# Adding the last bias to the residual in the middle stage instead of the last, for 12 of 16 pairs

## Chip, cores and metric

One core of a Trainium2 chip runs the whole program. The metric is the device time of one execution in microseconds (us). The engines are named as in the profile: PE multiplies matrices, DVE, ACT and POOL (GpSimd) work on elements, SP issues most of the transfers. All data are fp32; several products run on fp32 split into a high and a low part.

## What is computed

The input x has 32 samples of 64 channels by 1024 positions. Two blocks follow each other, each adding a feed-forward network over a style-modulated convolution network to its input:

```python
x = x + ffn0(cond0(x, cond))          # ffn0: 64 experts of rank 16, top 16 by a router, softmax gates
x = x + ffn1(cond1(x, cond))          # ffn1: a linear layer with 4-bit weights

def cond(x, style, ...):              # four modulated convolutions of width 3:
    for i, typ in enumerate(('same', 'upsample', 'same', 'downsample')):
        x = layer(x, style, weights[i], biases[i], mod_w[i], mod_b[i], typ)
    return x

def ffn1(x, qweight, scales, zeros, bias):
    W = scales * nibbles(qweight) - zeros          # per output column
    return einsum('bsi,io->bso', x, W) + bias
```

The change is about the last line, `+ bias`, and the `x +` in front of it. The bias has 1024 values, one for each position, and is the same for all rows.

## The kernel before

Two samples make a pair: 128 rows (2 x 64 channels) by 1024 positions. There are 16 pairs and three stages.

The first stage (loop at L1347) computes `cond0` and the first half of `ffn0` of each pair and leaves the gated products in DRAM. The second, the middle stage (loop at L1412), turns the products of pair p+1 on PE (`turned_h`, L1070), multiplies those of pair p with the second expert matrix (`layer0b`, L1108; 48 matmuls of 512 columns for one pair, the last 16 of them with the difference tile `td`), and adds x. The result is `x1`, the input of the second block. It lies in an order split four ways by position, `(f j)`, position 4j+f standing at f*256+j, because the second convolution network needs it so. It goes to DRAM twice: whole to `x1d` (L1160) as the residual, and as four parts with differences to `x1e` (L1162, L1172) for the convolutions.

The last stage (loop at L1477) computes `cond1` for pair k+1 and k+2 beside the 4-bit product of pair k (`layer1`, L1194). For each pair `load_x1` (L1177) brings the residual back from `x1d` into a buffer `xb`. `with_bias` (L1183) then makes a second buffer `o` on POOL in one instruction of 128 x 1024 (L1187): residual plus bias, with the order turned back to plain. A one-element copy named `turn` (L1215) in front of it pins it behind a DVE instruction of the next pair's convolutions. At the end DVE adds the zeros' part to `o` (L1226) and scales each third of the product (L1228), POOL adds that to `o` (L1230), and `o` is stored.

What else the steps below touch:

- Buffers with the tag `w4` are [128, 1024] and there are three. In the middle stage they hold the loaded products `hg` and `x1`; in the last `xb` and `o`.
- Buffers with the tag `hi` are [128, 512], three too. `high` (L146) takes one whenever DVE cuts the high part of a tile: twice for each pair in the middle stage (`hh`, inside `split`, L915), twice in the last.
- `crossed` (L931) makes `td` on POOL (L935, 128 x 1024) from a pair's high and low parts. There is one such buffer, so that of pair p+1 can be written only when PE has ended pair p; it must be there when PE reaches the last third of pair p+1.
- `cv` is one large buffer that is cut by hand (L44 to L50). In the middle stage it first holds the second expert matrix (`braw`, 8 x 1024 columns), then the set-up of the second convolution network (`set1`, one step of it after each of the pairs 1 to 6), the residual x of the next pair (`load_residual`), and small tiles of `ends` (L449), which computes the outermost outputs of the second network after pairs 12 and 13. Its last 2 x 1152 columns, `fwv(0)` and `fwv(1)`, are the composed convolution weights, first used by the last stage's work at pair 14.
- The framework that builds the kernel orders each engine's instructions by its own estimate of when they are ready and by their place in the program; `tc.issue_after` pins one behind another. A buffer of a pool is given out when its first writer is placed, and the waits that this needs are added.

Of the kernel before, what the change touches and what calls it, by code (L numbers as in the profile page):

```python
# [8 lines left out]
F32 = mybir.dt.float32  # L9
# [3 lines left out]
ALU = mybir.AluOpType  # L13
AX = mybir.AxisListType

P = 128
# [4 lines left out]
NP = B // 2  # L21
L = 1024
# [3 lines left out]
H = 512  # L26
# [19 lines left out]
XD, XE, Y, FW = L + 4, 3 * HQ - 1, YE + 4 * P, 9 * P  # L46
O_XE = 2 * XD
O_Y = O_XE + 2 * XE
O_FW = O_Y + 2 * Y
CV = O_FW + 2 * FW  # L50
# [13 lines left out]
def adaln_ffn_kernel(ctx: ExitStack, tc: tile.TileContext, t, out: bass.AP):  # L64
    nc = tc.nc
# [25 lines left out]
    cv = const.tile([P, CV], F32, name="cv")  # L91
# [21 lines left out]
    eps = const.tile([P, 1], F32, name="eps")  # L113
    condT = const.tile([P, B], F32, name="condT")

    x1d = dram.tile([NP, P, 4, L // 4], F32, name="x1d")
    x1e = dram.tile([NP, P, 2, XE], F32, name="x1e")
    hgd = dram.tile([NP, P, L], F32, name="hgd")
    rowd = dram.tile([2, B, 2, C], F32, name="rowd")
# [2 lines left out]
    def xdv(n):  # L122
        return cv[:, (n % 2) * XD : (n % 2 + 1) * XD]
# [35 lines left out]
        return p > (4 if i == 0 else 1)  # L159

    DIRECT = 4


    def zeros_once():
# [489 lines left out]
                )  # L654
        return fw

    def clear(i):

        for n in range(2):
            if i == 0:  # L660
                nc.gpsimd.memset(xdv(n)[:, 0 : L + 3 : L + 2], 0.0)
            nc.gpsimd.memset(fwv(n)[C:, NT * C : 8 * C], 0.0)

    def clear_y(ys):
# [431 lines left out]
    def load_residual(p):  # L1096
        if p in WHOLE:
            v = tokens("tl", f"xres{p}", F32).rearrange("p a b -> p (a b)")
        elif p < NP - 1:
            v = cv[:, O_Y + Y : O_Y + Y + L]  # L1100
        elif p < NP:
            v = wk.tile([P, L], F32, tag="w4", name="xres", bufs=3)
        else:
            return
        nc.sync.dma_start(v, t["x"][p])
        residual[p] = v

    def layer0b(p, ws):  # L1108

        whole = p in WHOLE  # L1110
        key = f"h{p}"
        xres = residual.pop(p)
        x1 = wk.tile([P, L], F32, tag="w4", name=f"x1_{p}", bufs=3)
        x4 = x1.rearrange("p (f j) -> p j f", f=4)

        def banks(c):
            return [fpst(f"o{p}_{c}_{j}") for j in range(1 if whole else 2)]

        def joined(c, qd):
            cs = slice(c * H, (c + 1) * H)  # L1120
            v = xres[:, cs]
            if not whole:
                nc.vector.scalar_tensor_tensor(v, qd[1], -SCALING / RADIX, v, ALU.mult, ALU.add)  # L1123
            nc.vector.scalar_tensor_tensor(  # L1124
                x4[:, c * P : (c + 1) * P],
                qd[0].rearrange("p (j f) -> p j f", f=4),
                SCALING if whole else SCALING * (1.0 + 1.0 / RADIX),
                v.rearrange("p (j f) -> p j f", f=4),
                ALU.mult,
                ALU.add,  # L1130
            )

        cols = [slice(c * H, (c + 1) * H) for c in range(2)]
        if p == NP - 1:
            qds = [banks(c) for c in range(2)]

            for part in (Q, D):
                for k in range(4):
                    for ch in zip(qds, cols):
                        product(ch, key, ws, lambda k: k, part, (k,))  # L1140
            yield
            for ch in zip(qds, cols):
                product(ch, key, ws, lambda k: k, Q, range(4, NC))
                yield
            for c, ch in enumerate(zip(qds, cols)):
                product(ch, key, ws, lambda k: k, D, range(4, NC))
                joined(c, qds[c])
                if c == 0:
                    yield
        else:  # L1150
            qds = [banks(c) for c in range(2)]
            for ch in zip(qds, cols):
                product(ch, key, ws, lambda k: k, Q)
            for c, ch in enumerate(zip(qds, cols)):
                product(ch, key, ws, lambda k: k, D)
                joined(c, qds[c])
                yield
        if p not in WHOLE:
            load_residual(p + 1)
        nc.sync.dma_start(x1d[p].rearrange("p f j -> p (f j)"), x1)  # L1160
        v = x1.rearrange("p (f j) -> p f j", f=4)
        nc.sync.dma_start(x1e[p, :, :, : HQ - 1], v[:, :2])  # L1162
        dd = wk.tile([P, 4 * HQ], F32, tag="rt", name=f"dd{p}", bufs=1)
        dd = dd.rearrange("p (f j) -> p f j", f=2)
        nc.gpsimd.memset(dd[:, :, 0:1], 0.0)
        nc.vector.tensor_tensor(dd[:, :, 1:HQ], v[:, 2:], v[:, :2], ALU.subtract)
        nc.scalar.mul(dd[:, :, HQ : HQ + 1], v[:, :2, 0:1], -1.0)
        done["dd"] = nc.vector.tensor_tensor(
            dd[:, :, HQ + 1 : 2 * HQ - 1], v[:, 2:, : HQ - 2], v[:, :2, 1 : HQ - 1], ALU.subtract
        )  # L1170
        nc.scalar.copy(dd[:, :, 2 * HQ - 1 :], v[:, 2:, HQ - 2 : HQ - 1])
        nc.sync.dma_start(x1e[p, :, :, HQ - 1 :], dd)  # L1172
        v = x1.rearrange("p (f j) -> p j f", f=4)
        for s, js in enumerate((slice(0, 2), slice(L // 4 - 2, L // 4))):
            nc.gpsimd.tensor_copy(xg[:, p, s].rearrange("p (j f) -> p j f", f=4), v[:, js])

    def load_x1(p):  # L1177
        if p < NP:
            v = wk.tile([P, L], F32, tag="w4", name=f"xb_{p}", bufs=3)
            nc.sync.dma_start(v, x1d[p].rearrange("p f j -> p (f j)"))  # L1180
            residual[NP + p] = v

    def with_bias(p, aux):  # L1183

        if p < NP:
            o = residual[p] = wk.tile([P, L], F32, tag="w4", name=f"o1_{p}", bufs=3)
            nc.gpsimd.tensor_tensor(  # L1187
                o.rearrange("p (j f) -> p j f", f=4),
                residual.pop(NP + p).rearrange("p (f j) -> p j f", f=4),
                aux[:, 2].rearrange("p (j f) -> p j f", f=4),  # L1190
                ALU.add,
            )

    def layer1(p, wq, aux):  # L1194


        o = residual.pop(p)
        for c in range(3):
            if c == 0:
                load_x1(p + 1)  # L1200
            ps = fpst(f"q{p}_{c}")[:, :QC]
            for j, half in enumerate(toks[f"x1_{p}"]):
                for k in range(NC):
                    nc.tensor.matmul(  # L1204
                        ps,
                        half[:, k],
                        wq[at(k)][:, c * QC : (c + 1) * QC],
                        start=(k == 0 and j == 0),
                        stop=(k == NC - 1 and j == 1),
                    )  # L1210
                if j == 0:
                    if c == 1 and p + 1 < NP:

                        turn = tiny.tile([P, 1], F32, tag="turn", name=f"turn{p}")
                        v = nc.gpsimd.tensor_copy(turn, uppers[f"h1_{p + 1}_0"][:, :1])  # L1215
                        with tc.issue_after(v.ins):
                            with_bias(p + 1, aux)
                    yield
            a = 2 if c == 0 else 0
            cs = slice(c * QC + a - 2, (c + 1) * QC - 2)  # L1220
            if c == 0:
                nrs = tiny.tile([P, 1], F32, tag="nrs", name=f"nrs{p}")
                nc.vector.tensor_scalar_mul(nrs, ps[:, 0:1], -1.0)
            if c == (0 if p == NP - 1 else 2):
                with tc.issue_after(done["lo"].ins):
                    nc.vector.scalar_tensor_tensor(o, aux[:, 1], nrs, o, ALU.mult, ALU.add)  # L1226
            s = wk.tile([P, QC], F32, tag="yt", name=f"sc{p}_{c}", bufs=2)[:, : QC - a]
            nc.vector.tensor_tensor(s, ps[:, a:], aux[:, 0, cs], ALU.mult)  # L1228
            eng = nc.vector if p == NP - 1 and c == 2 else nc.gpsimd
            eng.tensor_tensor(o[:, cs], o[:, cs], s, ALU.add)  # L1230
            if p == NP - 1:
                nc.sync.dma_start(out[p][:, cs], o[:, cs])
            yield
        if p < NP - 1:
            nc.sync.dma_start(out[p], o)
# [66 lines left out]
            split_weights(araw, AW, (k,), wa, "wa")  # L1302

    nc.sync.dma_start(condT, t["condT"])
    clear(0)
    zeros_once()
    set0 = factors(0, *(block(k, [P, 3 * AW], F32, f"room{k}") for k in range(2)))
    next(set0)
# [103 lines left out]
    for p in range(NP):  # L1412
# [9 lines left out]
            begin(NP + 1)  # L1422
        if p <= len(WHOLE):
            load_residual(p)
        main = layer0b(p, braw if p in WHOLE else wb)
        next(main)
        if p in WHOLE:
            split_weights(braw, L, range(4 * p, 4 * p + 4), wb, "wb")
        if p == 7:
            clear(1)  # L1430
            clear_y([yv(0)])
        if p == LAST:
            load(NP)
            tables_of(NP)
            set_ends = ends(1, 0, LAST, cv[:, O_FW:])
        if p in (LAST, LAST + 1):
            next(set_ends)
        if p == NP - 2:
# [24 lines left out]
        run(main)  # L1463
        if p + 1 < NP:
            crossed(f"h{p + 1}")
        if 0 < p < 7:
            with tc.issue_after(done["td"].ins):
                next(set1, None)
# [75 lines left out]
```

## Time and profile before

| | us |
|---|---|
| median of 3 runs (lowest to highest) | 893.91 (893.53 to 894.51) |
| the profiled execution: span from its first to its last instruction | 893.1 |
| first stage, about | 0 to 407 |
| middle stage, about | 407 to 628 |
| last stage, about | 628 to 893 |

| busy us in | PE | DVE | ACT | POOL |
|---|---|---|---|---|
| 407 to 628 (221.0) | 217.2 | 162.3 | 72.4 | 84.0 |
| 628 to 893.1 (265.1) | 257.2 | 247.4 | 97.0 | 215.0 |

Times within the span are counted from its start. The page's first part gives each engine's busy time over the whole span. A table by windows gives it for stretches that one chooses, for instance one pair of a stage. The timeline lists instructions in order of time, with the idle time of the engine just before one, and what ended that, in square brackets. The 16 transfers of `x1d` out and the 16 back move 512 KB each.

### The profile page before, as it was taken

Reading aid. Unit: us, or ns where it says so; the run is one execution under the profiler, and the core shown is the slowest. Engines: PE = TensorE matmul, PEld = TensorE weight load, DVE = VectorE, ACT = ScalarE, POOL = GpSimd, SP = SyncE. Lnnn points to the kernel's source line nnn. Section 1 sums busy time; section 2 is a strip of 40 time slices with the busy share of each in tenths; the row PEclk is TensorE's granted clock in tenths of the full one; section 3 lists DMA queues with packets and bytes.
Section 4 is the critical chain, followed back from the end, with each engine's and each line's share of the span. In section 5 each row is a group of like instructions: output and inputs, shape, how many; then the busy total and the mean of one; then the engine's idle time right before and its main releaser. Section 6 shows DMA issues by size and latency. Waiting matters only on the chain.

```text
span 893.1 us, 14916 instructions
## 1 busy us (share of the span) xinstructions
PE 866.1 (97%) x5033; PEld 775.1 (87%) x5033; DVE 723.2 (81%) x1460; ACT 352.4 (39%) x817; POOL 531.1 (59%) x745
## 2 busy tenths in 40 slices
PE   6989999999999999999999999999999999999997
PEld 4876888999999999994688888888899999999997
DVE  4475898888888888778986765669999999999996
ACT  6444544444444444333332221247333433343340
POOL 7235654666666666556572222343787888888884
PEclk9999999999999999999999999999999999999999
DMA  8632222222232222345475666555543334334321
GB/s 240 155 73 54 54 69 62 88 89 80 79 91 83 81 79 71 106 178 149 139 232 193 201 193 197 189 192 167 164 117 111 98 100 143 114 90 139 122 66 71
DMA packets 49739, 109.81 MB, mean 123 GB/s; under 512 B 13700, under 2 KB 22400, under 8 KB 49664
## 3 DMA queue, kind: packets, MB, share of 16 engines
q1 hardware_dynamic: 48704, 107.88, 39.5%
q10 hardware_dynamic: 960, 0.99, 0.5%
q8 instruction: 40, 0.66, 0.3%
q14 instruction: 35, 0.29, 0.1%
HBM read 70.97 MB, written 37.88 MB: 122 GB/s over the span
## 4 chain that ended last, share of the span: by engine, by line
PE 42%; DVE 7%; POOL 2%; issue 2%; ACT 0%; DVEq 0%; POOLq 0%; ACTq 0%
PE o L955 16%; PE q L1204 11%; PE f L619 3%; PE r L875 3%; PE c L773 2%; PE r L834 1%; PE r L843 1%; PE c L768 1%; PE ht L1079 1%; PE g L596 1%; DVE cv L716 1%; DVE x L1124 1%; PE p L826 1%; DVE rt L866 1%; DVE r L884 0%
## 5 line engine op out<-in xcount | busy, mean ns | idle before, releaser
L716 DVE TENSOR_TENSOR cv<-cv 128x257 f32<-128x257 f32 x120 | 105.8, 913 | 1.3 <-ACT cv L758 0.9
L730 POOL TENSOR_TENSOR cv<-cv 128x256 f32<-128x256 f32 x120 | 77.7, 647 | 29.8 <-DVE cv L716 25.1
L722 POOL TENSOR_TENSOR cv<-cv 128x128 f32<-128x128 f32 x100 | 39.0, 411 | 67.5 <-PE r L843 48.3
L1204 PE MATMUL q<-wq,thx 128*128 128x342 f32 x384 | 73.0, 332 | 2.1 <-ACT thx L913 2.1
L955 PE MATMUL h<-wa,tdx 128*128 128x352 f32 (+1 forms) x336 | 72.2, 351 | 0.2 <-DVE wa L382 0.2
L1204 PE MATMUL q<-wq,tlx 128*128 128x342 f32 x384 | 72.3, 330 | 0.0
L619 PE MATMUL f<-gs,iw 128*128 128x128 f32 (+1 forms) x384 | 68.2, 327 | 0.1
L619 PEld LDWEIGHTS f<-gs,iw 128*128 128x128 f32 x384 | 61.8, 190 | 5.9 <-issue 0.5
L955 PE MATMUL h<-wa,thx 128*128 128x352 f32 (+1 forms) x336 | 64.7, 333 | 0.0
L1204 PEld LDWEIGHTS q<-wq,thx 128*128 128x128 f32 x384 | 60.3, 189 | 4.1 <-ACT thx L913 3.2
L770 ACT ACTIVATE yt<-c,be,al 128x257 f32<-128x257 f32 x56 | 31.7, 567 | 80.4 <-PE c L768 77.3
L875 PE MATMUL r<-cv 128*128 128x128 f32 x480 | 63.4, 274 | 0.0
L1204 PEld LDWEIGHTS q<-wq,tlx 128*128 128x128 f32 x384 | 61.9, 189 | 0.8
L955 PE MATMUL h<-wa,tlx 128*128 128x352 f32 (+1 forms) x336 | 62.4, 327 | 0.0
L955 PE MATMUL o<-wb,thh 128*128 128x512 f32 x224 | 60.4, 402 | 1.5 <-ACT wb L375 1.5
L935 POOL TENSOR_TENSOR tdx<-thx,tlx 128x1024 fp32r<-128x1024 f32 x14 | 34.7, 2479 | 44.5 <-ACT tlx L927 36.2
L955 PEld LDWEIGHTS h<-wa,tdx 128*128 128x128 f32 x336 | 56.9, 188 | 2.4 <-DVE wa L382 0.5
L1123 DVE SCALAR_TENSOR_TENSOR cv<-o,cv 128x512 f32<-128x512 f32 x26 | 18.0, 692 | 50.2 <-PE o L955 50.2
L955 PE MATMUL o<-wb,tlh 128*128 128x512 f32 x224 | 58.4, 397 | 0.0
L875 PEld LDWEIGHTS r<-cv 128*128 128x128 f32 x480 | 58.4, 191 | 0.0
L634 ACT COPY cv<-f 128x256 f32<-128x256 f32 x64 | 24.0, 375 | 83.9 <-PE f L619 46.3
L642 POOL TENSOR_TENSOR cv<-cv 128x256 f32<-128x256 f32 x60 | 50.0, 833 | 11.4 <-ACT cv L637 11.4
(313 smaller groups left out, 2274.6 us busy)
## 6 DMA issues: line engine op xcount, KB each, us to landing
cv<-in_x_dram SPq DMA_DIRECT2D x60, 256.0 KB
cv<-x1e SPq DMA_DIRECT2D x64, 192.5 KB
x1e<-dd SPq DMA_DIRECT2D x16, 514.0 KB
hgd<-hs SPq DMA_DIRECT2D x16, 512.0 KB
hg<-hgd SPq DMA_DIRECT2D x16, 512.0 KB
x1d<-x SPq DMA_DIRECT2D x16, 512.0 KB
xb<-x1d SPq DMA_DIRECT2D x16, 512.0 KB
out_dram<-o SPq DMA_DIRECT2D x15, 512.0 KB
```

The source lines that it names most:

```text
L619: done["f"] = nc.tensor.matmul(pv[:, n : n + 2 - k], iw[:, e].rearrange("p a b -> p (a b)"), v, start=(m == 0), stop=(m == len(steps) - 1) ...
L634: nc.scalar.copy(f8[:, 0::2], pv[:, :, h])
L642: nc.gpsimd.tensor_tensor(f[:, 4 * P : 6 * P].rearrange("p (a b) -> p a b", b=P), v[:, :, 0], v[:, :, 1], ALU.add,)
L716: nc.vector.tensor_tensor(d[:, k], yo[:, k : k + HQ], yb, ALU.subtract)
L722: nc.gpsimd.tensor_tensor(y[:, YB + k * P : YB + (k + 1) * P], y[:, 2 * k : 2 * k + 2 * P - 1 : 2], y[:, 1 : 2 * P : 2], ALU.subtract,)
L730: nc.gpsimd.tensor_tensor(e[:, :, k], d[:, :, 2 * k : 2 * k + HQ - 2 : 2], d[:, :, 1 : HQ - 1 : 2], ALU.subtract,)
L770: nc.scalar.activation(yt, mid, AF.Identity, bias=be0[:, n : n + 1], scale=a)
L875: done["r"] = nc.tensor.matmul(ps[:, j * P : (j + 1) * P], y[:, YE + (2 * q + k) * P : YE + (2 * q + k + 1) * P], w(q + 2 * k), start=True ...
L935: done["td"] = nc.gpsimd.tensor_tensor(*(v.rearrange("p a b -> p (a b)") for v in (td, *toks[key])), ALU.subtract)
L955: nc.tensor.matmul(banks[l == 2], toks[key][l][:, order(k)], w[:, cols], start=(k == first and l != 1), stop=(k == last and l in (2, min(n ...
L1123: nc.vector.scalar_tensor_tensor(v, qd[1], -SCALING / RADIX, v, ALU.mult, ALU.add)
L1204: nc.tensor.matmul(ps, half[:, k], wq[at(k)][:, c * QC : (c + 1) * QC], start=(k == 0 and j == 0), stop=(k == NC - 1 and j == 1),)
```

## The change

For the pairs 2 to 13 (`early`) the bias is added in the middle stage. `bias` becomes a view of the last 1024 columns of `cv`, loaded once at pair 2. After each pair's `crossed`, `store_biased` adds the bias to the two halves of `x1` on POOL, turning the order back to plain, into two buffers of the tag `hi`, and each is stored into its half of `x1d`. The whole store of `x1` to `x1d` is left out for these pairs. In the last stage the loaded buffer is then the residual with bias itself: `with_bias` does nothing for them, its `turn` is left out, and no second buffer is taken. Pairs 0, 1, 14 and 15 go as before. The small tiles of `ends` move to other columns of `cv`, and a clearing of part of `fwv` at pair 7 is left out (the one after pair 13 remains).

```diff
-    x1d = dram.tile([NP, P, 4, L // 4], F32, name="x1d")
+    x1d = dram.tile([NP, P, L], F32, name="x1d")
...
+    bias = cv[:, CV - L :]
+
+    def early(p):
+
+        return len(WHOLE) <= p < NP - 2
...
-    def clear(i):
+    def clear():
 
         for n in range(2):
-            if i == 0:
-                nc.gpsimd.memset(xdv(n)[:, 0 : L + 3 : L + 2], 0.0)
+            nc.gpsimd.memset(xdv(n)[:, 0 : L + 3 : L + 2], 0.0)
             nc.gpsimd.memset(fwv(n)[C:, NT * C : 8 * C], 0.0)
...
-        nc.sync.dma_start(x1d[p].rearrange("p f j -> p (f j)"), x1)
+        if not early(p):
+            nc.sync.dma_start(x1d[p], x1)
...
+        stored.append((p, x4))
+
+    stored = []
+
+    def store_biased():
+
+        p, x4 = stored.pop()
+        if not early(p):
+            return
+        for c in range(2):
+            cs = slice(c * H, (c + 1) * H)
+            v = wk.tile([P, H], F32, tag="hi", name=f"xs{p}_{c}", bufs=3)
+            nc.gpsimd.tensor_tensor(
+                v.rearrange("p (j f) -> p j f", f=4),
+                x4[:, c * P : (c + 1) * P],
+                bias[:, cs].rearrange("p (j f) -> p j f", f=4),
+                ALU.add,
+            )
+            nc.sync.dma_start(x1d[p][:, cs], v)
 
     def load_x1(p):
         if p < NP:
             v = wk.tile([P, L], F32, tag="w4", name=f"xb_{p}", bufs=3)
-            nc.sync.dma_start(v, x1d[p].rearrange("p f j -> p (f j)"))
-            residual[NP + p] = v
+            nc.sync.dma_start(v, x1d[p])
+            residual[p if early(p) else NP + p] = v
 
     def with_bias(p, aux):
 
-        if p < NP:
+        if p < NP and not early(p):
...
-                    if c == 1 and p + 1 < NP:
+                    if c == 1 and p + 1 < NP and not early(p + 1):
...
+        if p == len(WHOLE):
+            nc.sync.dma_start(bias, t["bias"].partition_broadcast(P))
...
         if p == 7:
-            clear(1)
             clear_y([yv(0)])
...
-            set_ends = ends(1, 0, LAST, cv[:, O_FW:])
+            set_ends = ends(1, 0, LAST, cv[:, O_Y + Y + L : CV - L])
...
         if p + 1 < NP:
             crossed(f"h{p + 1}")
+        store_biased()
```

More of the change, by code (lines that the diff above doesn't have):

```diff
@@ L1304, in adaln_ffn_kernel @@
     nc.sync.dma_start(condT, t["condT"])
-    clear(0)
+    clear()
     zeros_once()
```

## Prediction

> **What bounds the kernel now.** I read the page's busy times first, then a table by windows, one for each pair, then the timeline where PE or DVE sat idle. Over the span PE is the fullest engine:
>
> ```profile
> PE 866.1 (97%) x5033; PEld 775.1 (87%) x5033; DVE 723.2 (81%) x1460; ACT 352.4 (39%) x817; POOL 531.1 (59%) x745
> ```
>
> POOL, whose work the change moves, is busy 59% on average, but 215.0 of 265.1 us in the last stage against 84.0 of 221.0 us in the middle one. That makes the move look worth much. The windows of the last stage, one pair each (columns: us, then busy us of PE, its weight loads, DVE, ACT, POOL), say otherwise:
>
> ```profile
> 654.05:671.77 17.72, 17.72 (x119) 17.13 (x119) 17.08 (x35) 6.93 (x18) 15.27 (x20) 1.00 0.38 113
> 671.77:690.20 18.43, 18.11 (x120) 17.17 (x120) 17.73 (x37) 6.93 (x18) 14.19 (x20) 1.00 0.35 108
> 690.20:708.72 18.52, 17.80 (x119) 16.91 (x118) 17.81 (x37) 6.93 (x18) 14.49 (x20) 1.00 0.35 108
> 708.72:726.44 17.72, 17.72 (x120) 17.12 (x119) 17.08 (x35) 7.00 (x18) 15.57 (x20) 1.00 0.38 114
> 743.60:760.67 17.07, 17.07 (x114) 16.47 (x113) 16.44 (x32) 6.92 (x18) 14.48 (x20) 1.00 0.38 117
> ```
>
> The last row is the steady pair: PE busy 17.07 of 17.07 us. Whatever leaves POOL there ends nothing sooner. In the first and fourth row PE has six small extra matmuls of `ends` (0.76 and 0.74 us in the timeline) and is still full. Only in the second and third is DVE, with 2.2 us of `ends` of its own, the later one:
>
> ```profile
> 684.81 0.67 PE L773 MATMUL c<-cv 128*128 128x256 f32 x2 [0.32 <-DVE rt L866]
> 703.49 0.67 PE L773 MATMUL c<-cv 128*128 128x256 f32 x2 [0.72 <-DVE rt L866]
> ```
>
> From 645 to 851 us these are PE's only waits: 206.00 less 204.96 busy, 1.04 us. The middle stage is bounded the same way: plain pairs take 11.79 us (PE's turns start at 506.94, 518.73, 530.51) with PE full, and DVE waits 4.2 us for PE in each:
>
> ```profile
> 517.11 0.69 DVE L1123 SCALAR_TENSOR_TENSOR cv<-o,cv 128x512 f32<-128x512 f32 x1 [4.19 <-PE o L955]
> ```
>
> **Removed in the last stage.** Twelve L1187 of 2.906 us and twelve `turn` of 0.186 us: 12 x 3.09 = 37.1 us of POOL, for pairs 2 to 13, that is those at 651 to 842 us. The four others stay, with the DVE stretches beside them at 628, 637, 859 and 876 us. What it does for PE goes through DVE:
>
> ```profile
> 646.00 0.75 DVE L716 TENSOR_TENSOR cv<-cv 128x257 f32<-128x257 f32 x2
> 756.94 2.91 POOL L1187 TENSOR_TENSOR o<-xb,aux 128x1024 f32<-128x1024 f32 x1
> 758.71 2.48 DVE L716 TENSOR_TENSOR cv<-cv 128x257 f32<-128x257 f32 x2
> ```
>
> Two L716 take 0.75 us alone and 2.48 beside L1187. Without it they may still meet the L1230 that comes next, as the pair of them at 662.26 us did (1.35 us). So DVE gains between 2.48 - 1.35 = 1.1 and 2.48 - 0.75 = 1.7 us a pair. In the two DVE-late pairs that brings its 17.73 and 17.81 us to 16.7 at most, below the 17.72 us that PE needs with `ends`. The gain is at least the visible waits, 1.04 us, and at most the excess, 18.43 + 18.52 - 2 x 17.72 = 1.51 us, since PE's busy time is stretched there too (18.11 against 17.72). I take 1.3, the middle. Elsewhere the 1.1 to 1.7 us are DVE idle time: cover is PE's full 17.07 us. L1226 and L1230 now work in the loaded buffer; one `w4` less a pair is taken, so its load can only go earlier.
>
> [...]
>
> **Added in the middle stage.** Per pair, two POOL adds of 128 x 512. Nearest rows: half an L1187, with the same strided turn, 1.45; L374, a 128 x 512 add, 1.27 at its shortest. I take 1.45, so 24 x 1.45 = 34.9 us. POOL has room: after `td` it idles some 8 us a plain pair. The first add needs x1's first half (ready 507.14 in the pair that PE ends at 507.0), yet stands behind `td` (507.35 to 509.74) in the program; so adds at about 509.8 and 511.3. They can hold L1166 and L1168 (509.91, 510.52) by up to 2 x 1.45 = 2.9 us, less than DVE's 4.2 us of idle time; cost 0. Were that cover gone, the rest would delay L1123 and L1124, which free a product bank 0.6 us before PE wants it (518.92 against 519.51). So it is in the two pairs with set-up work on DVE, which idles 2.07 us before 454.34 and 2.18 before 467.71: 2.9 less these and less 0.6 leaves 0.2 and 0.1 us. POOL is busy there already and DVE's hold with it, so I take 0 and keep 0.3 as the upper end. If the first add goes ahead of `td`, `td` ends at 511.2, and PE needs it at 515.10.
>
> Queued behind the adds on POOL is the set-up of the second network, and behind that the next `td`. There the cover is thin, once:
>
> ```profile
> 450.31 6.88 POOL L252 TENSOR_TENSOR cv<-cv 128x256 f32<-128x256 f32 x6
> 460.99 2.40 POOL L935 TENSOR_TENSOR tdh<-thh,tlh 128x1024 fp32r<-128x1024 f32 x1
> 465.69 3.79 PE L955 MATMUL o<-wb,tdh 128*128 128x512 f32 x16
> ```
>
> POOL works without a gap from 445.66 to 463.5. Pair 2's adds come in front and shift this `td` by 2.9 us, to end at 463.39 + 2.9 = 466.3; PE wants it at 465.69: a stall of 0.6 us. With 1.27 us an add it is 0.2; with pair 3's adds in front as well, 0.6 + 2.9 = 3.5; if the adds are placed behind the set-up, 0. I take 0.6, as the program puts pair 2's adds before the set-up and pair 3's after the `td`.
>
> **Transfers.** SP issues two stores of 256 KB for one of 512: bytes unchanged, 12 more issues of some 0.4 us on a queue that sleeps for 5 us a pair (511.36 + 0.89 to 517.58). Its stores wait for POOL until about 512.8; behind them is the `hg` load, issued at 517.58 and used at 530.51. The load of the bias (512 KB) can go when the last L374 has read that part of `cv`, at 436.4, and is needed at 448.4. Cost 0. [...] The rows of SP show several in flight, with nothing on PE waiting for them.
>
> The stores free the `hi` buffers late. A burst that starts at 509.5 has landed by 518.3 (the clearing of `dd` that waits for it is at 518.33). If DVE's second `hh` (511.12) had to take an add's buffer, DVE would stand still. But buffers are not taken in turn: the load of the third residual went out at 653.95, as soon as the second was read, before the second result was stored from the buffer next in turn:
>
> ```profile
> 653.95 0.33 SPq L1180 DMA_DIRECT2D xb<-x1d  x1
> 663.02 0.36 SPq L1235 DMA_DIRECT2D out_dram<-o  x1
> ```
>
> Live together are two adds and one `hh`, which three buffers hold. Cost 0, but see the rivals. The moved `ends` tiles and the clearing (0.15 us of POOL) cost nothing: `ends`' POOL steps (569.75 to 572.0) feed PE at 577.21, so 2.9 us in front of them still fit.
>
> **Sum.** -1.3 + 0.6 = -0.7 us against a span of 893.1; nothing outside the span is shown, and the median of the runs is 0.8 above it. So 893.91 - 0.7 = 893.2. Its own range: most gain without a stall, -1.5, to least gain with both stalls, -1.04 + 0.6 + 0.3 = -0.1, and 0.5 on either side for the spread of the runs shown: 891.9 to 894.3.
>
> **Rivals.** (1) Faster: the last stage loosens more, PE gets all 1.5 us, the stall of 0.6 does not come, and PE's wait of 0.41 us at 868.01 (for DVE's split, still beside an L1187) goes as DVE runs up with more slack: -1.9, 892.0. For it: DVE 96% busy. Against: full PE; the often hoped-for 12 x 1.7 = 20 us has no place to appear.
> (2) Slower, POOL's backlog: at 456 to 466 us pair 3's adds also come before the `td`. Price 3.5 - 1.3 = +2.2, 896.1. It decides from the point where that `td` starts after 463.3. For it: x1's first half of pair 3 is ready at 456.2. Against: the program's order.
> (3) Slower, the stores: DVE waits for a landing. If that is at 517.2 (one 256 KB store before the end of the burst), `hh` and its partner end at 518.5, L1123 and L1124 at 520.3, 0.8 us after PE's 519.51; for 11 pairs +8.8, with the sum above 902.0. At 516.3 it is nothing. Against: the free buffer shown above.
>
> **Numbers.** Forecast 0.50, (1) 0.19, (2) 0.19, (3) 0.12. I take 0.2% (1.8 us) as what a measurement can tell. The forecast counts as same, (1) as faster, (2) and (3) as slower: 0.19, 0.50, 0.31. Range 891.7 to 896.8: all but (3) and the edges of (1) and (2).
>
> **What would show it.** In the profile after: L1187 four times; steady last-stage pairs still 17.07 us with DVE at 14.7 to 15.3; the pairs at 672 to 709 near 17.7; plain middle pairs 11.79; one PE wait on `td` near 465. I am wrong if middle pairs lengthen, with DVE `hh` waiting for a transfer, or if a pair of the last stage takes less than 17.07.

## The result, and the profile after

| | us: median (lowest to highest) | ratio to before, 95% interval |
|---|---|---|
| before, beside it | 894.13 (893.53 to 894.51) | |
| after | 898.21 (896.78 to 900.80) | 1.0045 (1.0033 to 1.0057) |
| after, measured again | 899.25 (897.90 to 900.51) | 1.0055 (1.0042 to 1.0068) |

The changed kernel is slower by some 4 to 5 us. The forecast was 893.2, and the upper end of its range 896.8. The profiled execution of after has a span of 895.3 us and took 897.11. Its busy times, first part of the page:

```profile
PE 862.7 (96%) x5033; PEld 772.8 (86%) x5033; DVE 739.8 (83%) x1460; ACT 352.4 (39%) x817; POOL 537.8 (60%) x743
```

DVE is 16.6 us busier than before (723.2), though none of its instructions is new: the same 1460 take longer. POOL is 6.7 busier: the 24 additions take 41.5 us (1.53 to 2.03 each) in the middle stage, and what they replace in the last took 37.1. Six executions differ more than before's do: the three with a granted clock of 1.000 took 896.78 to 897.18 us, the three at 0.994 to 0.998 took 899.24 to 900.80. Windows of one pair each in the last stage of after (us, then busy us and count of PE, its weight loads, DVE, ACT, POOL, then granted clock, DMA share, GB/s), at the places of the second, third and fifth row shown of before:

```profile
674.41:692.35 17.94, 17.94 (x121) 17.05 (x120) 16.46 (x35) 6.92 (x18) 10.91 (x16) 1.00 0.36 110
692.35:710.71 18.36, 17.95 (x120) 17.04 (x120) 17.66 (x37) 6.92 (x18) 11.60 (x17) 1.00 0.35 110
745.59:762.65 17.06, 17.06 (x113) 16.46 (x113) 15.65 (x32) 7.04 (x18) 11.38 (x18) 1.00 0.45 137
```

POOL has given up its 3 us a pair, and the steady pair is as long as it was. Only the first of the two DVE-late pairs is freed; the second is still 0.41 us longer than PE's work. What PE waits for, from its timeline in after:

```profile
461.10 0.23 PE L350 MATMUL rows<-ident,cv 64*32 64x64 f32 x1 [1.61 <-DVE cv L283]
467.00 3.92 PE L959 MATMUL o<-wb,tdh 128*128 128x512 f32 x16 [0.43 <-POOL tdh L939]
585.42 0.27 PE L562 MATMUL rt<-ident,cv 128*48 128x128 f32 x1 [1.90 <-DVE cv L471]
705.63 0.67 PE L777 MATMUL c<-cv 128*128 128x256 f32 x2 [0.41 <-DVE rt L870]
```

The first three are new and lie in the middle stage. The last is what is left of before's 0.32 and 0.72. The set-up, timeline of before, DVE and PE:

```profile
458.44 0.68 DVE L1166 TENSOR_TENSOR dd<-x 128x512 f32<-128x512 f32 x1
459.04 0.89 DVE L1168 TENSOR_TENSOR dd<-x 128x510 f32<-128x510 f32 x1
459.85 0.94 DVE L278 RECIPROCAL cv<-cv 128x128 f32<-128x128 f32 x1
459.86 1.30 PE L955 MATMUL o<-wb,tlh 128*128 128x512 f32 x5
461.09 0.23 PE L345 MATMUL rows<-ident,cv 64*32 64x64 f32 x1
```

And of after, POOL, DVE and PE:

```profile
445.19 1.56 POOL L1193 TENSOR_TENSOR xs<-x,cv 128x512 f32<-128x512 f32 x1
...
450.48 1.60 POOL L1193 TENSOR_TENSOR xs<-x,cv 128x512 f32<-128x512 f32 x1
...
452.44 7.19 POOL L257 TENSOR_TENSOR cv<-cv 128x256 f32<-128x256 f32 x6
...
457.06 1.30 DVE L1171 TENSOR_TENSOR dd<-x 128x512 f32<-128x512 f32 x1
458.28 1.91 DVE L1173 TENSOR_TENSOR dd<-x 128x510 f32<-128x510 f32 x1
458.86 0.63 PE L959 MATMUL o<-wb,tlh 128*128 128x512 f32 x2
460.11 0.94 DVE L283 RECIPROCAL cv<-cv 128x128 f32<-128x128 f32 x1
...
463.05 1.56 POOL L1193 TENSOR_TENSOR xs<-x,cv 128x512 f32<-128x512 f32 x1
464.56 2.38 POOL L939 TENSOR_TENSOR tdh<-thh,tlh 128x1024 fp32r<-128x1024 f32 x1
```

Pair 2's two additions push the six steps L257 back, from 450.31 to 457.19 before to 452.44 to 459.63 here. There they lie beside DVE's two differences `dd`, which take 1.30 and 1.91 us where before they took 0.68 and 0.89. The reciprocal stands behind them in DVE's order: it starts 3.98 us after its pair's first turn `ht` (456.13), before 2.72 us (457.13). The transpose `rows` stands behind it in PE's order, and earlier than it did: behind two of the eight `tlh` products, where it stood behind five. An estimate from these rows: the reciprocal is 1.3 us later, the three products (a quarter of a us each) make 0.7, and before `rows` had 0.3 to spare, which leaves 1.7, about the wait of 1.61. Then pair 3's first addition goes in front of `td` as well.

The transpose of `ends` shows the mechanism most plainly. Timeline of before, around it:

```profile
580.09 2.37 POOL L935 TENSOR_TENSOR tdh<-thh,tlh 128x1024 fp32r<-128x1024 f32 x1 [0.17 <-PE o L955]
...
582.17 0.35 DVE L466 TENSOR_TENSOR cv<-cv,bep 128x48 f32<-128x48 f32 x1
...
582.67 0.27 PE L557 MATMUL rt<-ident,cv 128*48 128x128 f32 x1
```

And of after:

```profile
581.04 1.53 POOL L1193 TENSOR_TENSOR xs<-x,cv 128x512 f32<-128x512 f32 x1
...
582.86 2.35 POOL L939 TENSOR_TENSOR tdh<-thh,tlh 128x1024 fp32r<-128x1024 f32 x1
583.01 2.27 DVE L471 TENSOR_TENSOR cv<-cv,bep 128x48 f32<-128x48 f32 x1
```

Before, `td` is at its end when DVE comes to this small step. After, one addition (with two clearings in `fwv` of 0.15 us each) has shifted `td` so that it starts 0.15 us ahead of the step, and the step lasts until `td` is done: 2.27 us for an instruction of 0.35. Against `ht`, at 580.92 before and 581.76 after, `td` starts 1.9 us later and the step at the same place. The transpose `rt` (585.42, above) waits for it, and all of PE's queue behind `rt`.

The plain pairs of the middle stage hold their 11.79 us. DVE's cover there, in its timeline of after, has shrunk to as little as 1.14 us, where before has 4.62 and 4.63 at the same two places:

```profile
529.74 0.69 DVE L1127 SCALAR_TENSOR_TENSOR cv<-o,cv 128x512 f32<-128x512 f32 x1 [1.14 <-PE o L959]
541.53 0.69 DVE L1127 SCALAR_TENSOR_TENSOR cv<-o,cv 128x512 f32<-128x512 f32 x1 [2.31 <-PE o L959]
```

And two `hh` did wait for a store, by the waits of DVE (us in all, times, longest):

```profile
DVE hh L149 <- DMA x1d<-xs: 6.3, 2, 5.0
```

PE's turns `ht` and steps `f` mark the same places in every kernel here. The table has by how much each stretch is longer than in before's profile (us of before's span; the first 398 us differ by -0.9 to +1.2 between executions, for kernels that are the same there, so they are left out):

| kernel | 398 to 469, set-up | 469 to 507 | 507 to 581 | 581 to 636, `ends` | 636 to 863, last stage |
|---|---|---|---|---|---|
| after | +2.28 | -0.59 | 0 | +1.94 | -0.63 |
| after_again | +2.26 | -0.62 | 0 | +3.54 | -0.62 |
| only_7_11 | 0 | 0 | 0 | +0.15 | -0.03 |
| late_7_13 | 0 | -0.04 | 0 | +1.93 | 0 |
| behind_td | +3.62 | 0 | +3.90 | +0.85 | -0.65 |
| only_2_11 | +2.26 | -0.04 | 0 | +0.11 | -0.61 |
| middle_only | +2.29 | +0.34 | +2.17 | +2.01 | 0 |
| last_only | -0.12 | -0.05 | 0 | -0.03 | -0.62 |
| gap_ends | -0.14 | 0 | -0.09 | +0.75 | 0 |
| adds_13 | -0.11 | 0 | 0 | +3.55 | 0 |
| adds_2_3 | +2.28 | 0 | 0 | +0.14 | +0.07 |
| ends_later | -0.12 | -0.02 | 0 | -0.03 | 0 |
| early_ends_later | +0.02 | 0 | 0 | +0.16 | -0.68 |

After: 2.28 - 0.59 + 1.94 - 0.63 = +3.0 us, from the three new waits, less the 0.6 gained in the last stage and less 0.6 of a wait that before has at 496 us (0.53, for `rows`) and after has not. These 3.0 are what the three executions at a clock of 1.000 show (2.7 to 3.1 over before's median).

### The profile page after: what moved, and what is told of

The parts are those of the page before. It is cut to its first block, busy times and chain, and to the rows that moved or that the text cites. A ratio compares the mean times of both kernels' runs of the same rounds, so it can differ in the third digit from the quotient of the medians.

```text
span 895.3 us, 14923 instructions
## 1 busy us (share of the span) xinstructions
PE 862.7 (96%) x5033; PEld 772.8 (86%) x5033; DVE 739.8 (83%) x1460; ACT 352.4 (39%) x817; POOL 537.8 (60%) x743
## 4 chain that ended last, share of the span: by engine, by line
PE 76%; DVE 11%; POOL 6%; issue 4%; ACT 2%; DMA 1%; ACTq 0%; SPq 0%; DVEq 0%; POOLq 0%
PE h L959 18%; PE o L959 16%; PE q L1228 11%; PE f L624 6%; PE r L879 5%; PE c L777 5%; PE r L838 3%; PE g L601 2%; PE r L847 2%; PE c L772 2%; PE p L830 1%; PE ht L1083 1%; POOL wa L379 1%; DVE wah L149 1%; DVE cv L720 1%
## 5 line engine op out<-in xcount | busy, mean ns | idle before, releaser
L734 POOL TENSOR_TENSOR cv<-cv 128x256 f32<-128x256 f32 x120 | 77.5, 646 | 29.8 <-DVE cv L720 25.1
L720 DVE TENSOR_TENSOR cv<-cv 128x257 f32<-128x257 f32 x120 | 93.7, 813 | 1.3 <-ACT cv L762 1.0
L647 POOL TENSOR_TENSOR cv<-cv 128x256 f32<-128x256 f32 x60 | 54.2, 904 | 25.3 <-ACT cv L642 25.3
L1254 POOL TENSOR_TENSOR xb<-xb,sc 128x342 f32<-128x342 f32 (+1 forms) x36 | 34.7, 965 | 38.5 <-DVE sc L1252 38.5
```

Of the source, the lines that this page charges most:

```text
L647: nc.gpsimd.tensor_tensor(f[:, 4 * P : 6 * P].rearrange("p (a b) -> p a b", b=P), v[:, :, 0], v[:, :, 1], ALU.add,)
L720: nc.vector.tensor_tensor(d[:, k], yo[:, k : k + HQ], yb, ALU.subtract)
L734: nc.gpsimd.tensor_tensor(e[:, :, k], d[:, :, 2 * k : 2 * k + HQ - 2 : 2], d[:, :, 1 : HQ - 1 : 2], ALU.subtract,)
```

## The experiments

Three theories. **A, held queues:** the additions hold DVE instructions beside them (the two `dd` above, 1.30 and 1.91 us for 0.68 and 0.89) and push `td` and the set-up back; PE waits where its order has a transpose behind them. **B, held buffers:** the stores keep the buffers of `hi`, and DVE waits (the prediction's third rival). **C, the clock:** a new PE wait is, in some executions, followed by a lower granted clock, which makes PE's work behind it longer. Beside the first four runs before took 893.98 us (893.28 to 895.67), beside the next four 894.34 (893.11 to 896.39), beside the last four 894.76 (893.33 to 896.28).

**The changed kernel again.**

> The changed kernel once more, unchanged. Theory A (held queues): the same PE waits at the same places, 1.6 us at the set-up's transposition near 461 us, 0.4 us for td near 467 and 1.9 us at the transposition of the ends near 585; span near 895.3 in executions with a granted clock of 1.000. Theory C (clock): the executions differ by the granted clock alone; those below 0.999 are 2 to 4 us longer, and the executions of the kernel before do not show this.

899.25 us, the same three waits (1.40, 0.47 and 1.90 us). The stretch of `ends` is 1.6 us longer than in the first profile, with the same wait in it. Windows of 5 us from 583 on, after_again (columns as above):

```profile
583.00:588.00 5.00, 3.10 (x20) 2.56 (x21) 4.57 (x6) 0.46 (x2) 4.86 (x5) 0.94 0.54 150
588.00:593.00 5.00, 5.00 (x17) 3.92 (x17) 4.02 (x5) 2.11 (x3) 1.07 (x1) 0.72 0.59 219
```

The same stretch, 1.8 us earlier, in the first profile of after:

```profile
581.00:586.00 5.00, 3.02 (x21) 2.51 (x22) 4.57 (x6) 0.46 (x2) 4.86 (x6) 1.00 0.48 142
586.00:591.00 5.00, 5.00 (x23) 4.12 (x22) 4.25 (x5) 1.88 (x3) 1.30 (x1) 1.00 0.57 214
```

The granted clock is 0.94 and 0.72 in the one, 1.00 in the other, and the eight `tlh` products behind the wait take 2.65 us (at 589.39) and 2.00 (at 586.68). An estimate from the windows: (0.06 + 0.28) x 5 = 1.7 us of PE's time. The five executions are ordered by their clock, from 897.90 at 0.999 to 900.51 at 0.994. But such a dip is no mark of the new waits alone, as I expected it to be: before's own profile has one, behind two short waits for the second expert matrix. Timeline of PE and windows of before:

```profile
430.87 0.50 PE L955 MATMUL o<-wb,thh 128*128 128x512 f32 x1 [0.63 <-ACT wb L375]
432.28 0.50 PE L955 MATMUL o<-wb,thh 128*128 128x512 f32 x1 [0.91 <-ACT wb L375]
430.00:435.00 5.00, 3.46 (x11) 2.36 (x10) 5.00 (x5) 3.63 (x11) 4.94 (x6) 0.79 0.48 146
435.00:440.00 5.00, 5.00 (x21) 4.08 (x20) 3.82 (x5) 2.12 (x5) 2.22 (x11) 0.87 0.00 0
```

After has the same waits (0.59 and 0.93) at a clock of 1.00. The dip costs before little: the next wait, of 1.08 us for DVE's L1127 at 443.99 in after, does not occur in it, and the set-up stretch of kernels without the dip and without additions there is 0.11 to 0.14 us shorter.

**Only the plain pairs.**

```diff
-        return len(WHOLE) <= p < NP - 2
+        return 7 <= p < NP - 4
```

> The bias is added early only for pairs 7 to 11, away from the set-up (pairs 2 to 6) and from the ends (pairs 12, 13). Theory A: the middle stage shows no PE wait that the kernel before lacks; the last stage waits for DVE again as before (0.3 and 0.7 us); time within 0.1% of the kernel before, about 894. Theory B (DVE waits for stores that hold its scratch buffers): plain pairs suffer as well, 896 or more.

894.77 us, ratio 1.0008 (0.9999 to 1.0017): no difference shown. Its profile has no new PE wait and no wait of DVE for a store. Five early pairs cost PE next to nothing (+0.15 in the table), and gain nothing: the last stage's 0.32 and 0.71 stand at 684 and 703 us, at other pairs than these.

**Pairs 7 to 13.**

```diff
-        return len(WHOLE) <= p < NP - 2
+        return 7 <= p < NP - 2
```

> Early for pairs 7 to 13: set-up spared, ends not. Theory A: the waits near 461 and 467 us are gone, the one of 1.9 us at the transposition of the ends stays: about 1.9 us above the kernel before, 896. Theory B: 896 too, but with DVE waiting for transfers in the middle stage. Theory C: no change against the changed kernel, 897 to 898.

897.18 us, ratio 1.0033 (1.0020 to 1.0046). One new wait, in its timeline of PE:

```profile
583.83 0.27 PE L562 MATMUL rt<-ident,cv 128*48 128x128 f32 x1 [1.90 <-DVE cv L471]
```

So pairs 12 and 13, beside `ends`, bring the wait of 1.90; theory B, for which they would be like all others, does not explain it, and no `hh` waits for a store here. The last stage gains nothing here: the gain belongs to the first early pairs.

**The additions put behind `td`.**

```diff
-        store_biased()
+        with tc.issue_after(done["td"].ins):
+            store_biased()
```

> The changed kernel with both adds of a pair pinned behind that pair's td on POOL. Theory A: td comes as early as before, so the wait for td (0.4 us) and the one at the ends (1.9 us) go, and the one near 461 us (1.6 us), which comes from POOL's set-up work and the adds of pair 2, stays or shrinks: 2.3 us less than the changed kernel, about 895 to 896. Theory B: the adds' stores go later still, DVE waits for them longer: not faster than the changed kernel.

901.75 us, ratio 1.0083 (1.0069 to 1.0097): slower than the changed kernel, against what I expected. The wait at `rt` is gone, but PE waits elsewhere, among others:

```profile
461.95 0.23 PE L350 MATMUL rows<-ident,cv 64*32 64x64 f32 x1 [2.08 <-DVE cv L283]
...
569.13 0.93 PE L496 MATMUL ye<-cv,cw 128*128 128x120 f32 x6 [0.69 <-DVE cv L488]
573.00 0.88 PE L515 MATMUL ue<-cv,cu 128*128 128x120 f32 x6 [1.09 <-DVE cv L471]
```

Behind `td` the two additions come in a row, beside the `dd`, which take 1.31 and 1.90 us at 457.90 and 1.24 and 2.04 at 474.59. The hold was moved, not taken away. DVE waits for transfers here, too: 2.3 us in 4 times for the stores at `hh`, 2.9 us in 3 times at L1127 for the load of x, so neither the +3.62 nor the +3.90 is shown to be theory A's alone; their parts were not separated. In the 5 us from 460 on, in which the 2.08 us end, the granted clock was 0.71, which is part of the +3.62.

**Pairs 2 to 11.**

```diff
-        return len(WHOLE) <= p < NP - 2
+        return len(WHOLE) <= p < NP - 4
```

> As the changed kernel, but pairs 12 and 13 keep their bias in the last stage, so that no addition stands in front of the POOL work for pair 13's turn beside the steps of `ends`. Theory A (held queues: the additions hold DVE's two-input instructions and delay `td`, and PE waits at the two transposes): the wait of 1.90 us at the transpose `rt` of `ends` is gone, the waits at `rows` (1.4 to 1.6) and `td` (0.4) near 461 to 469 stay, the last stage keeps its shorter wait (0.4 us in place of 0.32 + 0.72): about 896.3 us, 2 under the changed kernel. Theory B (the stores hold the buffers of `hi`, in every middle pair): ten of twelve pairs still store, so 897.5 to 898.5. Theory C (a PE wait is followed, in some executions, by a stretch of lower granted clock that costs about 1.6 us): the spread of the runs narrows and the runs with a clock under 0.998 become fewer, because one wait fewer is left.

897.25 us, ratio 1.0027 (1.0018 to 1.0035). The table has the wait at `rt` gone (+0.11 for +1.94), set-up and last stage as in after: theory A's place. The -0.04 hides a further wait of 0.27 us for `td` at 481.07 against the 0.6 given back at 496. The size, 2.9 us over before, is above the trace's 2.26 - 0.04 + 0.11 - 0.61 = 1.7. I expected 896.3. Of the 1.2 between, 0.4 lies outside the span: time less span is 2.2 us in every execution of this kernel and 1.8 in those of before.

**The middle stage alone.** The additions go to a tensor that nothing reads; the last stage is before's.

```diff
-        if not early(p):
-            nc.sync.dma_start(x1d[p], x1)
+        nc.sync.dma_start(x1d[p], x1)
...
-            nc.sync.dma_start(x1d[p][:, cs], v)
+            nc.sync.dma_start(x1s[p][:, cs], v)
```

> The additions and stores of the middle stage are made as in the changed kernel, but into a tensor that nothing reads; the old store and the last stage are as before. Theory A: the three PE waits (`rows` 1.4 to 1.6, `td` 0.4, `rt` 1.9) stand, and the last stage keeps its 0.32 and 0.72: 0.65 us over the changed kernel, some 898.5 to 899.5. Theory B: one more store a pair on the same queue would make DVE's waits for the stores longer than the 6.3 us (2 waits, one of 5.0) of the changed kernel; with more of them reaching PE it would be above 900. The last stage's steady pairs: 17.06 us, as in both kernels, POOL back at 14.5 busy.

902.53 us, ratio 1.0085 (1.0069 to 1.0102). The three waits are there and the last stage is before's, as theory A has it, but there are waits for `td` of 0.35 to 0.67 more. Timeline of middle_only, POOL and PE:

```profile
474.63 0.10 POOL L1170 MEMSET dd<- 128x2 f32 x1 [6.09 <-DMA x1e<-dd]
...
475.33 2.00 POOL L1193 TENSOR_TENSOR xs<-x,cv 128x512 f32<-128x512 f32 x1
477.30 2.37 POOL L940 TENSOR_TENSOR tdh<-thh,tlh 128x1024 fp32r<-128x1024 f32 x1
479.72 3.92 PE L960 MATMUL o<-wb,tdh 128*128 128x512 f32 x16 [0.67 <-POOL tdh L940]
```

POOL's clearing of `dd` waits for the store of the `dd` before it, and the addition and `td` stand behind the clearing. Counted from the pair's `ht`, the clearing comes at 2.93 us in after (no wait for this `td`), at 3.49 with pairs 2 to 11 alone (0.27) and at 3.90 here (0.67). DVE's `hh` waits for stores 11.0 us in 3 times. So a held buffer is real when the queue carries twice the stores, but it is `dd`, which theory B did not name, that reaches PE; in the changed kernel, with two waits of `hh` of 6.3 us in all, stores could reach PE at most inside the set-up, whose length the run without stores below settles.

**The last stage alone.** Before, without the bias for pairs 2 to 13 (`with_bias` and the `turn`).

```diff
-        if p < NP:
+        if p < NP and not 2 <= p < NP - 2:
```

> The kernel before, with the additions of the bias in the last stage left out for pairs 2 to 13 (their outputs lack the bias, and the small instruction that orders them is left out too); the middle stage is untouched. Prediction's step: 1.3 us shorter than before (892.6), with both waits of 0.32 and 0.72 gone. Theory A, from the changed kernel's trace: only 0.65 shorter (893.3), because one wait of 0.4 for the tile `rt` of the incoming conditioning steps stays. If neither, and the time is before's within 0.2, the last stage gives nothing back at all.

893.64 us, ratio 0.9989 (0.9980 to 0.9997): 0.7 us gained, 0.62 in the trace. Timeline of PE, last_only:

```profile
702.40 0.67 PE L773 MATMUL c<-cv 128*128 128x256 f32 x2 [0.41 <-DVE rt L866]
```

With all twelve additions gone, that is all that the last stage gives back.

**A gap without additions.** Before, with fourteen small DVE steps behind the last step of `ends`.

```diff
         with next_behind():
             scaled(rp, ps, 3)
+        if (i, lo) == (1, 0):
+            for _ in range(14):
+                nc.vector.tensor_scalar_mul(rp, rp, 1.0)
```

> The kernel before, with fourteen small DVE multiplications by 1.0 chained behind the last step of `ends` in the middle stage, so that the transpose `rt` on PE finds its operand some 1.5 to 2.5 us late, with no other work added to POOL, DVE or a queue. Theory A alone (a PE wait costs its own length): the time rises by the wait seen at `rt`, so 895.3 to 896.0 for a wait of 1.4 to 2. Theory C (a wait is followed by a stretch of lower granted clock in some executions): the runs fall into two groups, one at the wait's length and one about 1.6 us above it, the latter with a granted clock about 0.003 lower, and the median rises by more than the wait.

895.29 us, ratio 1.0009 (1.0000 to 1.0017). It does not answer the question, as the transpose stands later in PE's order here. Timeline of gap_ends, DVE and PE:

```profile
585.70 1.96 DVE L557 TENSOR_SCALAR cv<-cv 128x48 f32<-128x48 f32 x9
...
587.81 0.27 PE L560 MATMUL rt<-ident,cv 128*48 128x128 f32 x1
```

PE shows no wait before it: the framework, which counts these steps in its estimate, put 29 products between `ht` and `rt`, where there were 3 before. That the time lies at the lower edge of what I expected (895.3) is therefore luck. Of the 0.75 us of the stretch, 0.56 lies in two later waits of PE, at 609.55 (0.40) and 612.67 (0.16), which before has not.

**Pair 13's additions alone, no store.** As the middle stage alone, but for one pair, and the result is stored nowhere.

```diff
-        return len(WHOLE) <= p < NP - 2
+        return p == NP - 3
...
-            nc.sync.dma_start(x1d[p][:, cs], v)
```

> As the kernel before, with the two additions of pair 13 made a second time in the middle stage, ahead of `td` as in the changed kernel, into buffers that nothing reads: no store, no other pair, last stage as before. Theory A (held queues): `td` of the next pair starts one addition later, DVE's step of `ends` behind it is held to the end of `td` (2.3 us in place of 0.35), and PE waits 1.9 us for the transpose `rt`; everything before 580 us and the last stage as before: before + 1.9. Theory B (the buffers of `hi` held by stores): without a store nothing waits, before's time. Theory C (a PE wait is followed in some executions by a lower granted clock, some 1.6 us): the runs lie between before + 1.9 and before + 3.5, the median at about + 2.7, those with the lower clock on top.

897.24 us, ratio 1.0033 (1.0022 to 1.0043). Timeline of adds_13:

```profile
579.67 1.54 POOL L1192 TENSOR_TENSOR xs<-x,cv 128x512 f32<-128x512 f32 x1
...
581.50 2.35 POOL L939 TENSOR_TENSOR tdh<-thh,tlh 128x1024 fp32r<-128x1024 f32 x1
...
581.64 2.27 DVE L471 TENSOR_TENSOR cv<-cv,bep 128x48 f32<-128x48 f32 x1
...
584.06 0.27 PE L562 MATMUL rt<-ident,cv 128*48 128x128 f32 x1 [1.91 <-DVE cv L471]
```

One addition of 1.54 us ahead of `td` makes the whole wait; no store, no buffer, no other pair is needed. In this execution the clock falls after it, too (windows):

```profile
580.00:585.00 5.00, 3.09 (x21) 2.50 (x20) 4.57 (x6) 0.46 (x2) 4.86 (x5) 0.95 0.39 97
585.00:590.00 5.00, 5.00 (x17) 3.95 (x17) 3.87 (x5) 2.23 (x3) 1.02 (x2) 0.71 0.73 276
```

By the estimate above that is (0.05 + 0.29) x 5 = 1.7 us, and the stretch is 3.55 us longer instead of 1.94. The runs lie 1.6 to 3.9 us above before, the median 2.5, which is about the spread that theory C expected (1.9 to 3.5). Their order is not: the run at a clock of 1.000 took 897.04, and two at 0.997 and 0.998 took less.

**Pairs 2 and 3 alone, no store.** The same with `p in (2, 3)`.

> The same for pairs 2 and 3 alone, no store: the four additions beside the set-up. Theory A: POOL's set-up steps end 2.4 us later, DVE's `dd` and reciprocal wait with them, PE waits 1.4 to 1.6 us at `rows` and 0.4 at the turn that needs `td`; the wait of 0.53 at 496 us goes in exchange: + 2.3 - 0.6 = + 1.7. Theory B: before's time, there is no store. Theory C: some runs up to 1.6 above that, with a lower clock behind 461 us.

898.35 us, ratio 1.0041 (1.0027 to 1.0055). Timeline of PE:

```profile
461.23 0.23 PE L350 MATMUL rows<-ident,cv 64*32 64x64 f32 x1 [1.57 <-DVE cv L283]
467.14 3.93 PE L959 MATMUL o<-wb,tdh 128*128 128x512 f32 x16 [0.47 <-POOL tdh L939]
```

The set-up is longer by the 2.28 us of the changed kernel, with no store in it: theory B falls there. The 0.6 that I expected back at 496 us is not given back; in after it came from other pairs' additions, and which was not tried. The median, 3.6 above before, is 1.1 over the trace's 2.28 + 0.14 + 0.07 = 2.5; time less span is 0.2 us longer than before's, and the profiled execution, at a clock of 0.999, is the fastest of five, the others being at 0.995 to 0.998.

**A better place, and its control.** Early pairs 7 to 11, and the last stage's steps of `ends` beside pairs 5 to 9; the control has the second part alone, in the kernel before.

```diff
-        elif k < NP + 8:
+        elif NP + 4 < k < NP + 12:
             next(set_ends, None)
```

> The kernel before, with the steps of the last stage's `ends` made beside pairs 5 to 9 instead of 1 to 5; nothing of the bias is changed. Control for the next run. The last stage's two waits of PE for DVE's `rt` (0.32 and 0.72 at 685 and 703) move some 68 us later and keep their size: before's time within 0.3.

> Early bias for pairs 7 to 11 alone (plain pairs of the middle stage, where the additions cost PE nothing: its five period lengths were those of before), and the steps of the last stage's `ends` beside pairs 5 to 9, where the early pairs leave DVE unheld. If the gain of the last stage lies only where `ends` and the addition of the bias meet, its two waits of 0.32 and 0.72 become one of 0.41, as in the changed kernel and in the run without the bias: before - 0.65, 893.3. If the gain does not come from that meeting, before's time; if the plain pairs do cost something, above it.

Control 895.48 us, ratio 1.0005 (0.9997 to 1.0014); with the early pairs 894.40, ratio 0.9995 (0.9986 to 1.0004). I expected before's time within 0.3 and 893.3; both came out higher. In the traces the control's waits of 0.33 and 0.72 stand at 754 and 773 us, and with the early pairs one of 0.41 at 772 is left: the last stage is 0.68 us shorter with them and unchanged in the control, and the middle stage pays 0.16 at most. So the gain lies where the addition of the bias meets `ends`, and the trace has it almost free of cost; but 0.7 us of 894 is below what these runs can tell from nothing.

## Why the prediction was wrong

**The bound and the plain pairs: right.** Steady pairs of the last stage kept 17.06 us with POOL 3 us emptier, plain middle pairs 11.79.

**The gain of the last stage: right in kind, half the size.** "I take 1.3", with 1.04 at the least; it was 0.61 to 0.68 in six traces. The mis-sized term is "DVE gains between 2.48 - 1.35 = 1.1 and 2.48 - 0.75 = 1.7 us a pair". In the steady pair DVE's busy time fell from 16.44 to 15.65, 0.8 us; in the two DVE-late pairs by 17.73 - 16.46 = 1.27 and by 17.81 - 17.66 = 0.15. Two L716 that took 2.48 us beside L1187 at 688.63 take 1.48 in after (L720, at 691.10), beside the next POOL addition (L1254, at 691.26); the two at 700.02 take 1.61, where they took 1.35 at 698.13 before. So the next POOL instructions fill a part of the place, and the lower bound should have allowed for that.

**`td` at the set-up: right in size, by luck.** Forecast 0.6, measured 0.43. The order was that of the second rival: pair 3's first addition in front, `td` started at 464.56, behind the deciding 463.3. Its 3.5 us did not come, since PE itself was 1.6 us late by then. So two steps that the forecast did not have, the order and PE's lateness, nearly cancelled.

**The hold of DVE at the set-up: the first step that failed.** "2.9 less these and less 0.6 leaves 0.2 and 0.1 us ... I take 0 and keep 0.3 as the upper end." It was priced by the two additions beside DVE's idle time before L1123 and L1124 alone. But the additions also push POOL's own L252 (L257 after) beside `dd`, and behind `dd` stands the reciprocal that PE's `rows` waits for: 1.61 us in after, 1.57 with the additions of pairs 2 and 3 alone. That the framework would then place `rows` three products earlier was not foreseen either. An addition took 1.58 us in the median and up to 2.03, not the 1.45 taken.

**`ends`: the second step that failed, with the longer wait.** "`ends`' POOL steps (569.75 to 572.0) feed PE at 577.21, so 2.9 us in front of them still fit" looks for POOL's own work being late. It took the first addition to stand behind `td`, as in the program; the framework put it in front, here as in all the early pairs. And it does not ask what a `td` that starts 1.9 us later now lies beside. That was DVE's step L466 (L471 after), with the two inputs `cv` and `bep`, at the end of the chain to `rt`: 1.90 us. That a `td` can hold DVE is in before's own timeline, POOL and DVE:

```profile
599.48 2.87 POOL L935 TENSOR_TENSOR tdh<-thh,tlh 128x1024 fp32r<-128x1024 f32 x1
600.00 2.88 DVE L1168 TENSOR_TENSOR dd<-x 128x510 f32<-128x510 f32 x1
```

L1168 takes 0.68 us at its shortest. The forecast priced such a hold for the added instructions and L1166 and L1168, and not for the instructions that the additions shift.

**The stores: right for this kernel.** "Cost 0, but see the rivals": the wait of the third rival occurred twice (5.0 and 1.4 us on DVE), not in 11 pairs, and the cost of both places appears without any store. The margin is small: with pairs 2 to 11 alone a late store of `dd` goes with a wait of PE of 0.27 us, read from the trace and not tried apart. No cost of the twelve more transfers as such appears: the set-up is 2.28 us longer with the stores (after) and without (pairs 2 and 3 alone).

**The rest: not foreseen.** The trace's sum is +3.0; the medians are 4.1 and 5.3 above before. In the first measurement the executions at a clock of 1.000 keep to the sum, and those below it are 2 to 4 us longer. In after_again and adds_13 the clock fell behind the wait at `rt` and took 1.6 us more; in three other profiles with that wait (after, late_7_13, middle_only) it did not. That the wait causes the dip was not shown apart from the additions, as the gap kernel made no gap, and before's profile has a dip as well. For the kernels of pairs 2 to 11, and of 2 and 3, whose profiles have no such dip behind the new waits, 0.8 and 0.9 us within the span stay open; a dip in other executions would fit for pairs 2 and 3, but the executions of pairs 2 to 11 are not ordered by their clock.

## What to carry to other kernels

When work moves to an engine with room, price not only the moved instructions but what each instruction behind them will lie beside once it has moved: here an addition of 1.5 us shifted a 2.4 us one onto a small step of another engine, 2.27 us for 0.35, whose result PE's queue wanted next. The share of idle time said nothing of this; the pairs with extra work (set-up, `ends`) must be looked at one by one, on every engine. And the removal was worth only the waits it ended: 37 us of POOL's work removed from the last stage gave 0.6.

## What the hardware showed

In after and in adds_13 a small DVE instruction (L471, with the two inputs `cv` and `bep`) that started 0.14 to 0.15 us after POOL's `td` lasted to that one's end: 2.27 us for 128 x 48 values, ending at 585.28 with `td` at 585.21 in after, and at 583.91 with `td` at 583.85 in adds_13; in before, with 0.29 us of `td` left, it took 0.35. A larger one, `dd` of 128 x 512 at 446.91 in after, took 2.88 us (0.68 at its shortest) and ended at 449.79, 0.54 us behind the `td` that had started at 446.71.

The granted clock fell to 0.71 or 0.72 over 5 us behind PE waits of 1.90 and 1.91 us in two of five profiles with such a wait (after_again and adds_13), and cost, by the estimate above, about 1.7 us of PE's time each time. It was 0.71 also in the 5 us around the 2.08 of the additions put behind `td`, and 1.00 around each of the five waits of 1.40 to 1.61. No shortest wait follows from this: in before's profile the clock fell (0.79 and 0.87 over 5 us each from 430) at waits of 0.63 and 0.91 us, which ended at 430.87 and 432.28; the same estimate gives (0.21 + 0.13) x 5 = 1.7 us. What sets the dip off, and why it comes in one execution of the same kernel and not in another (0.72 in after_again, 1.00 in after), was not shown.
